# Layer 1's two inner PReLUs as max(y, alpha y) in one VectorE step instead of relu on ScalarE plus a VectorE step

## The chip, the cores and the metric

The kernel runs on one core of a Trainium2 chip. The metric is the device time of that core in microseconds, from repeated executions. All runs in this document gave correct results, and none was in the slow state, with one caveat: the single timed run of one experiment (an unchanged kernel, looked at once) has no known state. The profile is one further execution, taken with the hardware profiler, so its span (1042.2 us before) is near the timed median, not equal to it. The granted clock is the share of TensorE's full clock that the chip allowed, as the profiler recorded it; a drop is a fall of it from 1.00 to 0.50.

## The reference, cut to what matters

The program is four layers on 16 images of 256 channels and 28 x 28 pixels. Layer 0 is a binary convolution with batch norm, layer 2 has two binary convolutions, layer 3 is attention. The change is in layer 1 alone:

```python
def prelu(x, alpha):
    return jnp.where(x >= 0, x, _pc(alpha) * x)      # all alphas are 0.25 here

residual = prelu(x, a_alpha1)
z = hardsign(x + _pc(a_move))
y = conv3x3(z, a_w)                                   # cut
y = prelu(bn(y, a_bn1), a_alpha2)                     # inner PReLU 1
mix = s * x + y * (1.0 - s)
y = se_gate(mix, ...) * y
y = bn(y * residual, a_bn2) + residual
res2 = y
u = conv1x1(hardsign(y + _pc(f_move)), f_w)           # cut
u = prelu(bn(u, f_bn1), f_alpha2)                     # inner PReLU 2
mix2 = s2 * y + (1.0 - s2) * u
u = bn(se_gate(mix2, ...) * u, f_bn2)
return u + res2
```

`se_gate` needs the mean of each channel over the image: mean, a small product (below "hid"), relu, another small product ("gate"), sigmoid. So the gate of an image cannot be computed before the PReLU of all its channels is done.

## The kernel before

Channels lie on the 128 partitions in two blocks, so a block of an image is a tile of 128 x 784. The 16 images run through a software pipeline, `iteration(b)`: the 3x3 convolution of image b beside the gates, 1x1 convolution and second PReLU of images b-1 and b-2. In the traces TensorE, VectorE and ScalarE run in the order in which the program names their work: ScalarE's eviction, relu, eviction, relu of `unit_u` and `unit_r` at the end start in that order, 0.9 us apart, from about 484.3 us on before. The kernel has TensorE write a convolution's result to PSUM (tile "cv"); an eviction is the instruction that moves it out of there. The row step (L654) is VectorE's eviction of the 3x3 convolution, which makes y. Each PReLU is two instructions: ScalarE computes r = relu(-y), VectorE computes y + (1 - alpha) r and sums it for the gate.

```python
def relu_neg(ap, bias=0.0, scale=-1.0, apart=False):            # L569
    r = full("rn", "rn", 4)
    ...     # A.activation(r, ap, AF.Relu, bias=bias, scale=scale), in two halves if apart
    return r

def prelu_a(b, mo):
    pairs[b, mo] = relu_neg(ys[b, mo])

def prelu_b(b, mo):                                             # L664
    y = ys[b, mo]
    V.scalar_tensor_tensor(
        y, pairs.pop((b, mo)), ra2[:, mo:mo + 1], y, ALU.mult, ALU.add,
        accum_out=sums_of(b + 1)[1][:, 0, mo:mo + 1],
    )

def unit_u(b, mo, u=None, vector=False):                        # evicts the 1x1 convolution
    ...
    if vector:                                                  # L735
        for h in range(2):
            V.tensor_scalar(halves(u)[:, h], ps[:, h], s3[:, m], c3[:, m], ALU.mult, ALU.add)
    else:                                                       # L737
        A.activation(halves(u), ps, AF.Identity, bias=c3[:, m], scale=s3[:, m])
    us[b, mo] = (u, ps)

def unit_r(b, mo, apart=False):                                 # relu, from PSUM, beside the eviction
    ...
    us[b, mo] = (u, relu_neg(ps, nc3[:, m], ns3[:, m], apart))

def unit_b(b, mo):                                              # L747
    u, r = us[b, mo]
    V.scalar_tensor_tensor(
        u, r, rf2[:, mo:mo + 1], u, ALU.mult, ALU.add, accum_out=sums_of(b + 2)[1][:, 1, mo:mo + 1]
    )
```

After the last image there is no other image's convolution to hide behind, so the two gates of the last image lie bare. The kernel fills these stretches with dummy matmuls (`keep_busy(n)`, tile "unused", L371), so that TensorE does not go quiet. I call what follows the end of layer 1, with a first and a second stage:

```python
# first stage: last branch of iteration(b) of the last image
conv1x1(b - 1)
for k in range(2):
    unit_u(b - 1, k)
    unit_r(b - 1, k)
    unit_b(b - 1, k)
for i, u in enumerate((0, 3)):
    conv_pair(b, 1, i, u)
px = hidden_x(B)
rows_out(b, 1)
prelu_a(b, 1)
prelu_b(b, 1)
...
b = B - 1
keep_busy(14)
g = gates(hidden_b(B, hidden_a(B, px)))
keep_busy(14)
...                                     # product with the residual, sign, conv1x1(b)
# second stage
unit_u(b, 0, last[:, 0, :])
unit_u(b, 1, last[:, 1, :], True)
for k in range(2):
    unit_r(b, k, k == 1)
    unit_b(b, k)
keep_busy(14)
h = hidden_a(B + 1, px)
...                                     # sums for layer 2's batch norm
g = gates(h)[:, 1]
keep_busy(14)
...                                     # in all 26 dummies up to layer 2's first convolution (L285)
```

## Time and profile before

| | before |
|---|---|
| timed runs, median (range) | 1045.65 us (1045.01 to 1046.67, 3 runs) |
| span of the profile | 1042.2 us |
| layer 1 in the profile | about 140 to 515 us |
| one image's period in layer 1 | 21.9 us |
| the end of layer 1, from the last period's gate matmul (474.82) to layer 2's first matmul (515.11) | 40.29 us |

The prediction below shows the engine table, the periods, TensorE's waits and the chain. One more view belongs ahead of it: the groups of instructions by shape, with what the two inner PReLUs cost. The columns are line, engine, operation, out<-in and shapes, count, then total busy us and mean ns of one, then the idle time ahead of them on their engine and what ended it.

```profile
L664 DVE SCALAR_TENSOR_TENSOR y<-rn,ra,y 128x784 f32<-128x784 f32 x32 | 33.0, 1032 | 9.4 <-ACT rn L569 9.3
L569 ACT ACTIVATE rn<-cv,nc,ns 128x784 f32<-128x784 f32 x31 | 31.1, 1004 | 0.0
L747 DVE SCALAR_TENSOR_TENSOR u<-rn,rf,u 128x784 f32<-128x784 f32 x30 | 30.0, 1030 | 4.3 <-ACT rn L569 4.3
L569 ACT ACTIVATE rn<-y 128x784 f32<-128x784 f32 x32 | 27.1, 846 | 10.1 <-DVE y L654 10.1
```

There are about 58 us of relus on ScalarE in these two rows, and about 14 us in which VectorE stood still for them. Whether any of that sets the time is another question, because TensorE is the engine that is never free in the periods (busy for 21.91 of 21.91 us).

### The profile page before, as it was taken

What the parts mean: (1) busy time and instruction counts of PE and PEld (TensorE: products, weight loads), DVE (VectorE), ACT (ScalarE), POOL (GpSimd) and SP (SyncE); (2) the same over time, 40 slices, a digit from 0 to 9 for tenths busy, and PEclk for the clock granted to TensorE, in tenths of its full rate; (3) what the DMA queues carried; (4) which work ended last, traced back from release to release, by engine and by line L of the source; (5) the groups of instructions that cost most, each with busy time, mean ns of one, the idle gap of its engine ahead of it and who ended that gap; (6) DMA issues with size and microseconds to landing.
All of it is one profiled execution on the core that took longest, in us unless ns stands there. A gap on an engine that the chain in (4) does not pass through costs nothing.

```text
span 1042.2 us, 15026 instructions
## 1 busy us (share of the span) xinstructions
PE 1007.5 (97%) x5667; PEld 827.9 (79%) x5667; DVE 826.0 (79%) x1460; ACT 729.8 (70%) x1189; POOL 139.4 (13%) x147
## 2 busy tenths in 40 slices
PE   6999999999999999999999999999999999999995
PEld 6899979999999999997589997999844444444442
DVE  4987588999999999985688887888865777768665
ACT  6888745777777777675777785777676676766652
POOL 2000100000000000000100000000024354443531
PEclk9999999999999999999899999999999999999998
DMA  9755521222332223100464000000013435344312
GB/s 340 235 192 187 199 78 47 93 78 78 108 109 90 81 78 105 66 32 31 176 255 186 1 1 1 1 1 1 1 32 62 95 92 124 68 119 90 97 63 97
DMA packets 24359, 98.77 MB, mean 95 GB/s; under 512 B 3203, under 2 KB 6981, under 8 KB 24277
## 3 DMA queue, kind: packets, MB, share of 16 engines
q1 hardware_dynamic: 18644, 67.17, 18.5%
q0 software_dynamic: 5632, 30.54, 10.8%
q8 instruction: 47, 0.77, 0.3%
q14 instruction: 36, 0.29, 0.1%
HBM read 65.59 MB, written 32.11 MB: 94 GB/s over the span
## 4 chain that ended last, share of the span: by engine, by line
PE 82%; DVE 9%; ACT 6%; issue 1%; DMA 1%; SPq 0%; POOL 0%; ACTq 0%; POOLq 0%; DVEq 0%
PE cv L614 27%; PE cv L285 23%; PE sc L1218 8%; PE av L1239 8%; PE cv L720 4%; PE mi L1195 4%; PE sm L1281 2%; PE mi L1297 2%; DVE ab L296 1%; ACT ab L295 1%; DVE p L1016 1%; PE unused L371 1%; ACT t L294 1%; PE sm L1239 1%; DVE l_parts L515 1%
## 5 line engine op out<-in xcount | busy, mean ns | idle before, releaser
L285 PE MATMUL cv<-fpads,wpk 128*128 128x392 f32 x1728 | 336.6, 356 | 9.2 <-POOL l_fin L152 7.3
L285 PEld LDWEIGHTS cv<-fpads,wpk 128*128 128x128 f32 x1728 | 327.5, 192 | 12.1 <-POOL l_fin L152 7.3
L614 PE MATMUL cv<-vs,w 128*128 128x392 f32 x1536 | 301.1, 354 | 1.4 <-DVE vs L121 1.4
L614 PEld LDWEIGHTS cv<-vs,w 128*128 128x128 f32 x1536 | 287.1, 190 | 3.0 <-issue 1.8
L1222 ACT ACTIVATE es<-sc 128x784 f32<-128x784 f32 x112 | 87.3, 822 | 41.4 <-PE sc L1218 41.4
L296 DVE SCALAR_TENSOR_TENSOR ab<-ab,cv 128x392 f32<-128x392 f32 x96 | 53.9, 561 | 65.8 <-ACT ab L295 65.4
L1218 PE MATMUL sc<-q,keyswa 64*128 64x392 f32 x448 | 90.0, 513 | 0.9 <-ACT es L1222 0.9
L1016 DVE SCALAR_TENSOR_TENSOR p<-ab,vec 128x392 f32<-128x392 f32 x128 | 79.1, 618 | 2.2
L1239 PE MATMUL av<-es,v 128*64 128x392 f32 x448 | 80.8, 499 | 0.0
L294 ACT ACTIVATE t<-cv,rounding 128x392 f32<-128x392 f32 x96 | 55.4, 577 | 27.1 <-PE cv L285 25.6
L1218 PEld LDWEIGHTS sc<-q,keyswa 64*128 64x128 f32 x448 | 38.9, 186 | 44.0 <-issue 17.1
L1232 POOL TENSOR_TENSOR sum<-sum,es 128x784 f32<-128x784 f32 x32 | 67.2, 2101 | 3.1 <-ACT es L1222 0.6
L1239 PEld LDWEIGHTS av<-es,v 128*64 128x64 f32 x448 | 29.4, 136 | 47.3 <-issue 47.0
L121 DVE TENSOR_TENSOR vs<-pad 128x840 fp32r<-128x840 bf16 (+1 forms) x66 | 64.4, 999 | 0.1
L295 ACT ACTIVATE ab<-t,unrounding 128x392 f32<-128x392 f32 x96 | 59.8, 623 | 3.2
L1206 DVE COPY keyswa<-mi 64x392 f32<-64x392 f32 x31 | 16.3, 564 | 52.1 <-ACT q L1202 52.1
L760 POOL DMA_DIRECT2D x2d<-x x16 | 8.6, 536 | 359.4 <-DVE x L754 296.9
L1019 ACT ACTIVATE t<-ab 128x392 f32<-128x392 f32 x64 | 33.5, 523 | 26.6 <-DVE ab L296 26.6
L720 PE MATMUL cv<-z,fw 128*128 128x392 f32 x256 | 48.8, 342 | 0.7 <-ACT z L712 0.7
L737 ACT ACTIVATE u<-cv,c_bn,s_bn 128x784 f32<-128x784 f32 x30 | 30.1, 1005 | 24.4 <-PE cv L720 24.4
L720 PEld LDWEIGHTS cv<-z,fw 128*128 128x128 f32 x256 | 45.8, 188 | 1.5 <-ACT z L712 1.3
L1195 PE MATMUL mi<-p,wqk 128*128 128x392 f32 x124 | 45.3, 506 | 0.3 <-PE unused L371 0.2
(275 smaller groups left out, 1500.0 us busy)
## 6 DMA issues: line engine op xcount, KB each, us to landing
xs<-in_x_dram SPq DMA_DIRECT2D x30, 784.0 KB, 4.8
x2d<-x POOLq DMA_DIRECT2D x16, 784.0 KB, 3.6
out_dram<-p SPq DMA_DIRECT2D x15, 784.0 KB, 3.8
p<-x2d POOLq DMA_DIRECT2D x14, 784.0 KB, 6.9
p<-x2d SPq DMA_DIRECT2D x13, 784.0 KB, 6.9
n0d<-n POOLq DMA_DIRECT2D x16, 392.0 KB, 4.9
n<-n0d SPq DMA_DIRECT2D x16, 392.0 KB, 3.1
st<-in_w_dram SPq DMA_DIRECT2D x12, 384.0 KB, 6.5
```

What stands on the lines that cost most here:

```text
L121: V.tensor_tensor(o, a, b, op)
L285: T.matmul(pss[j][:, n // size, :HN].rearrange("p (a b) -> p a b", b=S), lhsT=w[:, n, t, :], rhs=pads[:, j // 2 % 2, k, r:r + HR, c:c + S] ...
L294: A.activation(t, ps, AF.Identity, bias=rounding, scale=1.0 / PACK)
L295: A.activation(ab[:, 1], t, AF.Identity, bias=unrounding)
L614: T.matmul(ps.rearrange("p (a b) -> p a b", b=S), lhsT=w[:, k, c, u, mo * P:(mo + 1) * P], rhs=vs[:, b % 2, u, k, :, c:c + S], start=(n == 0),
L720: T.matmul(ps[:, h, :HN], lhsT=w[:, k, mo * P:(mo + 1) * P], rhs=z2[b][:, k, h * HN:(h + 1) * HN], start=(k + i == 0), stop=(k + i == 2),)
L1016: V.scalar_tensor_tensor(p, y, alpha[:, mo:mo + 1], y, ALU.mult, ALU.max)
L1195: T.matmul(ps[:, h, :HN], lhsT=wqk[:, k, :], rhs=x[b][:, k, h * HN:(h + 1) * HN], start=(k == 0), stop=(k == 1))
L1218: T.matmul(ps[:, h, :HN], lhsT=chunk[rows], rhs=qs[b][rows], start=True, stop=True)
L1222: A.activation(e, ps[:, :, :HN], AF.Exp, scale=0.125)
L1232: (V if late else nc.gpsimd).tensor_tensor(sums[b, late], sums[b, late], e, ALU.add)
L1239: T.matmul(ps[64 * h:64 * h + 64, :HN], lhsT=w, rhs=e[:, h, :], start=start, stop=stop)
```

## The change

For alpha at most 1, y + (1 - alpha) relu(-y) is max(y, alpha y), which VectorE does in one instruction that reads y twice (L663 after, 1032 ns). ScalarE's 65 relus for the two inner PReLUs go. The intent is to take work from ScalarE, to take one hand-over between engines out of each PReLU, and to shorten the two bare stages at the end. For the last image's second block the eviction goes back from VectorE (two halves) to ScalarE. As max is wrong for alpha above 1, the alphas are added to the values that the kernel checks at run time, and the careful version of the program, which runs if the check fails, keeps the general form.

```diff
-    doubts = const.tile([P, 8 * B + 6], F32, name="doubts")
+    doubts = const.tile([P, 8 * B + 10], F32, name="doubts")
...
+                for i, n in enumerate(("a_alpha2", "f_alpha2")):
+                    nc.gpsimd.tensor_copy(doubts[:, 8 * B + 6 + 2 * i:8 * B + 8 + 2 * i], pv(n))
...
-            def prelu_a(b, mo):
-                pairs[b, mo] = relu_neg(ys[b, mo])
-
-            def prelu_b(b, mo):
-                ...
+            def prelu(y, alpha, beta, mo, total):
+
+                if careful:
+                    V.scalar_tensor_tensor(
+                        y, relu_neg(y), beta[:, mo:mo + 1], y, ALU.mult, ALU.add, accum_out=total
+                    )
+                else:
+                    V.scalar_tensor_tensor(y, y, pv(alpha)[:, mo:mo + 1], y, ALU.mult, ALU.max, accum_out=total)
...   (unit_u loses its vector form, unit_r goes, unit_b calls prelu; the calls of prelu_a and unit_r go)
                 unit_u(b, 0, last[:, 0, :])
-                unit_u(b, 1, last[:, 1, :], True)
-                for k in range(2):
-                    unit_r(b, k, k == 1)
-                    unit_b(b, k)
+                unit_b(b, 0)
+                unit_u(b, 1, last[:, 1, :])
+                unit_b(b, 1)
                 keep_busy(14)
```

More of the change, by code (lines that the diff above doesn't have):

```diff
@@ L462, in forward @@
             cc, zb2 = vtile("cc"), vtile("zb2")
-            ra1, ra2, rf2, ns1, ns3, nc3 = (vtile(q) for q in ("ra1", "ra2", "rf2", "ns1", "ns3", "nc3"))
+            ra1, ra2, rf2, ns1 = (vtile(q) for q in ("ra1", "ra2", "rf2", "ns1"))
             mix_x, mix_y, mix_c = (const.tile([P, 2, 2], F32, name=n) for n in ("mix_x", "mix_y", "mix_c"))
@@ L472, in constants @@
                 nc.gpsimd.tensor_copy(
-                    doubts[:, 8 * B:], vec[:, VECS.index("a1"):VECS.index("a3") + 1, :].rearrange("p i k -> p (i k)")
+                    doubts[:, 8 * B:8 * B + 6], vec[:, VECS.index("a1"):VECS.index("a3") + 1, :].rearrange("p i k -> p (i k)")
                 )
+                for i, n in enumerate(("a_alpha2", "f_alpha2")):
+                    nc.gpsimd.tensor_copy(doubts[:, 8 * B + 6 + 2 * i:8 * B + 8 + 2 * i], pv(n))
                 v = const.tile([P, 4, 2], F32, name="v_bn")
@@ L487, in constants @@
                     V.tensor_scalar(o, pv(q), -1.0, 1.0, ALU.mult, ALU.add)
-                for o, q in ((ns1, s1), (ns3, s3), (nc3, c3)):
-                    V.tensor_scalar(o, q, -1.0, None, ALU.mult)
+                V.tensor_scalar(ns1, s1, -1.0, None, ALU.mult)
                 tt(zb2, c2, pv("f_move"), ALU.add)
@@ L564, in full, with relu_neg @@
                 return ph.tile([P, N], F32, tag=tag, name=name, bufs=bufs)
-            def relu_neg(ap, bias=0.0, scale=-1.0, apart=False):
+            def relu_neg(ap, bias=0.0):
                 r = full("rn", "rn", 4)
-                for i in range(2) if apart else (slice(0, 2),):
-                    A.activation(
-                        r if len(ap.shape) == 2 else halves(r)[:, i], ap if len(ap.shape) == 2 else ap[:, i], AF.Relu,
-                        bias=bias, scale=scale,
-                    )
+                A.activation(r, ap, AF.Relu, bias=bias, scale=-1.0)
                 return r
@@ L657, in rows_out, with prelu_y @@
                     )
-            def prelu_a(b, mo):
-                pairs[b, mo] = relu_neg(ys[b, mo])
-            def prelu_b(b, mo):
-                y = ys[b, mo]
-                V.scalar_tensor_tensor(
-                    y, pairs.pop((b, mo)), ra2[:, mo:mo + 1], y, ALU.mult, ALU.add,
-                    accum_out=sums_of(b + 1)[1][:, 0, mo:mo + 1],
-                )
+            def prelu(y, alpha, beta, mo, total):
[5 more added lines that the diff above has]
+                    V.scalar_tensor_tensor(y, y, pv(alpha)[:, mo:mo + 1], y, ALU.mult, ALU.max, accum_out=total)
+            def prelu_y(b, mo):
+                prelu(ys[b, mo], "a_alpha2", ra2, mo, sums_of(b + 1)[1][:, 0, mo:mo + 1])
             def hidden_x(t):
@@ L727, in conv1x1, with unit_u @@
                     us[b, mo] = ps
-            def unit_u(b, mo, u=None, vector=False):
+            def unit_u(b, mo, u=None):
                 m, ps = slice(mo, mo + 1), us[b, mo][:, :, :HN]
@@ L732, in unit_u @@
                     u = full("yu", f"u{b}_{mo}", 6)
-                if vector:
-                    for h in range(2):
-                        V.tensor_scalar(halves(u)[:, h], ps[:, h], s3[:, m], c3[:, m], ALU.mult, ALU.add)
-                else:
-                    A.activation(halves(u), ps, AF.Identity, bias=c3[:, m], scale=s3[:, m])
-                us[b, mo] = (u, ps)
-            def unit_r(b, mo, apart=False):
-                m = slice(mo, mo + 1)
-                u, ps = us[b, mo]
-                us[b, mo] = (u, relu_neg(ps, nc3[:, m], ns3[:, m], apart))
+                A.activation(halves(u), ps, AF.Identity, bias=c3[:, m], scale=s3[:, m])
+                us[b, mo] = u
             def unit_b(b, mo):
-                u, r = us[b, mo]
-                V.scalar_tensor_tensor(
-                    u, r, rf2[:, mo:mo + 1], u, ALU.mult, ALU.add, accum_out=sums_of(b + 2)[1][:, 1, mo:mo + 1]
-                )
+                prelu(us[b, mo], "f_alpha2", rf2, mo, sums_of(b + 2)[1][:, 1, mo:mo + 1])
             def branch2(b, k, g):
@@ L754, in branch2 @@
                 V.scalar_tensor_tensor(
-                    v, us.pop((b, k))[0], g[:, k:k + 1], v, ALU.mult, ALU.add, accum_out=sum_x2[:, k, b:b + 1]
+                    v, us.pop((b, k)), g[:, k:k + 1], v, ALU.mult, ALU.add, accum_out=sum_x2[:, k, b:b + 1]
                 )
@@ L785, in iteration @@
                     unit_u(b - 2, 0)
-                if one:
-                    prelu_a(b - 1, 1)
                 if two:
-                    unit_r(b - 2, 0)
                     unit_u(b - 2, 1)
-                    unit_r(b - 2, 1)
                 if ahead:
@@ L794, in iteration @@
                 if one:
-                    prelu_b(b - 1, 1)
+                    prelu_y(b - 1, 1)
                 if ahead:
@@ L826, in iteration @@
                         branch1_a(b - 1, k, g[:, 0])
-                prelu_a(b, 0)
                 for i, u in enumerate((1, 2)):
@@ L833, in iteration @@
                     branch1_b(b - 1, 1)
-                prelu_b(b, 0)
+                prelu_y(b, 0)
                 if two:
@@ L856, in iteration @@
                         unit_u(b - 1, k)
-                        unit_r(b - 1, k)
                         unit_b(b - 1, k)
@@ L862, in iteration @@
                     rows_out(b, 1)
-                    prelu_a(b, 1)
-                    prelu_b(b, 1)
+                    prelu_y(b, 1)
                     return px
@@ L927, in forward @@
                 for k in range(2):
-                    products(x2[b][:, k, :], shift[:, k:k + 1], us[b, k][0], sum_uv[:, k:k + 1])
-                squares(us[b, 0][0], 0.0, sum_uu[:, 0:1])
+                    products(x2[b][:, k, :], shift[:, k:k + 1], us[b, k], sum_uv[:, k:k + 1])
+                squares(us[b, 0], 0.0, sum_uu[:, 0:1])
                 V.tensor_scalar(sum_uv, sum_uv, 2.0, None, ALU.mult)
@@ L939, in forward @@
                 g = gates(h)[:, 1]
-                squares(us[b, 1][0], 0.0, sum_uu[:, 1:2])
+                squares(us[b, 1], 0.0, sum_uu[:, 1:2])
                 keep_busy(14)
```

## The prediction

> **What bounds the kernel now.** I read the page's engine table first, then the busy time by stretches, cut at the pieces of the chain of waits, then TensorE's waits in layer 1, and last the chain itself at layer 1's end.
>
> The engine table (busy us, share of the span, instructions):
>
> ```profile
> PE 1007.5 (97%) x5667; PEld 827.9 (79%) x5667; DVE 826.0 (79%) x1460; ACT 729.8 (70%) x1189; POOL 139.4 (13%) x147
> ```
>
> TensorE is busy nearly all the time; ScalarE, from which the change takes work, is only third. But a share of the whole span hides stages, so I cut layer 1 (about 140 to 515 us) into its images. The chain shows the same four pieces of convolution every 21.9 us (9.2, 2.85, 6.81 and 2.39 us), and these are two of those periods and two stretches of the end (columns: length, busy PE, PEld, DVE, ACT, POOL, then granted clock, DMA share, GB/s):
>
> ```profile
> 319.21:341.13 21.92, 21.92 (x121) 21.85 (x122) 20.28 (x39) 16.32 (x23) 0.53 (x1) 1.00 0.28 92
> 363.04:384.95 21.91, 21.91 (x121) 21.84 (x122) 20.27 (x39) 16.33 (x23) 0.53 (x1) 1.00 0.27 93
> 480.00:500.00 20.00, 17.64 (x82) 12.31 (x83) 13.11 (x30) 12.47 (x19) 0.75 (x2) 0.91 0.10 40
> 500.00:515.00 15.00, 13.14 (x59) 6.89 (x58) 11.39 (x46) 11.54 (x22) 1.73 (x6) 0.89 0.44 163
> ```
>
> In a period TensorE is busy for the whole 21.9 us and its weight loads for 21.84; VectorE leaves 1.6 us free and ScalarE 5.6. Between 140 and 479 us TensorE's waits are one line:
>
> ```profile
> PE cv L614 <- DVE vs L121: 1.4, 1, 1.4
> ```
>
> That one is the stage's start. So in the steady part the change has nothing to win: no matmul waits for a PReLU. Only after 480 us does TensorE idle, run dummy matmuls (tile "unused") and lose clock. There the chain of waits (start, length, what) reads:
>
> ```profile
> 489.11 1.08 DVE y L654 x2
> ...
> 490.27 0.87 ACT rn L569
> 491.13 0.03 issue
> 491.16 1.05 DVE y L664 x2
> ...
> 492.65 0.62 PE hid L542 x4
> ...
> 494.47 4.73 PE unused L371 x14
> 499.20 2.88 PE cv L720 x16
> 502.07 0.03 issue
> 502.10 1.29 DVE last L735 x2
> 503.39 0.02 issue
> 503.41 1.25 ACT rn L569 x2
> 504.67 0.03 issue
> 504.69 1.05 DVE last L747 x2
> ...
> 506.35 0.59 PE hid L542 x4
> ...
> 508.14 7.32 PE unused L371 x26
> 515.46 6.84 PE cv L285 x36
> ```
>
> Here both relus (L569) lie on the path: one for the last image's first PReLU, one pair of halves for its second. Each stage then runs through the small gate matmuls and a block of dummies.
>
> [...] The trace has 846 (relu of y), 946 (relu of the residual, one pointer) and 1005 (eviction, two pointers). [...] each relu that goes is worth its row. [...] layer 3's PReLU is already (mult, max) with the same tensor in both places (L1182), 1027 ns for 784 elements; the form removed (L664, mult, add) is 1032. [...] the granted clock is 1.00 until 494 us, 0.50 from about 494.6 to 498.0 and again from about 508.3 to 511.7, both 3.4 us long [...]. Both follow stretches where TensorE has little but the gate matmuls, which are 2 columns wide.
>
> **The change part by part.** Removed on ScalarE: 32 relus of y (32 x 846 ns = 27.1 us) and 31 whole and 2 half relus of the 1x1 convolution (32.4 us), 59.5 of its 729.8 us. VectorE's PReLU stays one instruction of about 1030 ns plus its 82 ns accumulator read, 64 of them, now reading one tensor twice and alpha from the parameter table: no change. The last image's second channel block is evicted by ScalarE (about 1000 ns) and no longer by VectorE in two halves (1.29 us with their overlap). VectorE loses two 0.16 us constants, GpSimd gains two tiny copies, both inside layer 0. Compared engine by engine, TensorE's order is the same, ScalarE has 64 instructions fewer (65 relus go, one eviction comes) and VectorE 4 in each of the two program variants, careful and not, and the count of activation table loads is the same.
>
> Steady part: 59 us off an engine that nobody on TensorE waits for. VectorE's waits for relus there (6.8 us in front of L664) go too, again unseen: 0 us.
>
> End, first stage. The chain's step at 489.11 starts late because VectorE has to finish the previous image's second PReLU, itself held until 487.99 by ScalarE's run of eviction, relu, eviction, relu (four times 0.9 us from 484.37). Without the relus that PReLU is done by about 487.4, and the row step starts when the convolution ends, at 488.55 in place of 489.02: 0.45. Then 0.98 us, from the row step's end at 490.18 to the PReLU's start at 491.16, is the wait for the relu. Offered: 1.4. But TensorE's 14 dummies before the gate matmul run 488.39 to 491.59, so the gate matmul can move only from 492.65 to about 491.55: 1.1 us.
>
> End, second stage. From the 1x1 convolution's end (502.07) to the last PReLU's end (505.74) it is now 1.29 + 1.25 + 1.05 and gaps. After: eviction 1.0 + PReLU 1.03 + gaps, about 2.15 us, so 1.5 less. Again 14 dummies (501.90 to 505.10) hold the gate matmul: 506.35 becomes 505.10 relative to the convolution, 1.25 us.
>
> Sum with the clock behaving as now: 1.1 + 1.25 = 2.35 us. Everything behind (gate, square, table load, statistics) has the same order and shifts along.
>
> Clock. TensorE's quiet stretch before the dummies shrinks from 2.7 us (491.59 to 494.3) to about 1.7, and the second from 2.9 (505.1 to 508.0) to 1.65[...]. Elsewhere in this trace idle gaps of 1.38 (138.5 us) and 1.35 us (639.4) cost no clock. If no drop happens, the 14 dummies of 4.73 us take about 3.1, as their like does at 488.4 (3.20). The 1x1 convolution then waits for its input instead: its first half would be ready at 496.5 and its second at 497.5, so it ends about 499.8 rather than 502.07 and the gain up to there is 2.25, not 1.1. The 26 dummies of 7.32 us become 5.6 (at 216 ns), and the next layer's first matmul is then held by its two sign instructions, about 7.65 us after the gate matmul started, against 8.8 now: 1.15 more. With no drop at all the total is about 1.1 + 1.15 + 1.25 + 1.15 = 4.65 us. I take some 40% of that extra 2.3, because [...] some runs before may lack a drop as well: 2.35 + 0.9 = 3.2 us.
>
> **The rivals.** First: ScalarE's relief speeds up every period. The relus are 3.7 us of each 21.9, and if they held TensorE, 16 periods would give up to 59 us (986 us, faster by 5%). For it: VectorE does wait for them and has 93% load. Against it: TensorE's 21.91 of 21.91. I give it 1%. Second: the wait only changes its name; the dummies and the gate chain are fixed, and the freed 1.4 and 1.5 us vanish in them: about 1045 us. For it: dummies stand in both stages and I have already capped both gains by them; against it: both gate matmuls start over 1 us after their dummies end. Third: VectorE, now without pauses, becomes the bound, or its in-place PReLU straight after the row step waits for that step's writes. Its work per period stays at 20.3 us of 21.9, and it has one instruction fewer at the end, so at most some 0.1 us twice. Fourth: the clock drops stay but fall elsewhere: 1043.3.
>
> **Range and chances.** 1045.65 - 3.2 = 1042.4 us. The three runs before spread over 1.7 us, the clock adds up to 2.3 us, so 1040.0 to 1044.9 should hold it 8 times in 10. Two per cent is 21 us, nine times the sure part: faster 0.01, slower 0.005.
>
> **What would show it.** Periods still 21.91 us with TensorE at 21.91 while ScalarE falls to about 12.6; the relu rows L569 of y and of the convolution gone, the residual's 32 kept; VectorE's PReLU still near 1030 ns; the gate matmuls starting as the dummies end; layer 2's first matmul 2.3 to 4.7 us earlier; all later stages as long as before. Wrong: a period other than 21.9; a PReLU well over 1.03 us; a gate matmul still a microsecond behind its dummies; or a clock drop over a quiet stretch of 1.7 us, which would leave 2.35.

## The result, and the profile after

| | before | after |
|---|---|---|
| timed runs of one call, median (range, runs) | 1045.57 us (1045.01 to 1046.67, 4) | 1041.31 us (1038.64 to 1041.76, 4) |
| ratio, 95% interval | | 0.9953 [0.9934, 0.9971] |
| span of the profile | 1042.2 us | 1039.0 us |

The verdict is "same" (within 2%), with a real gain of half a per cent. Ratios in this document are the mean time of one kernel's fast runs over that of the other's fast runs of the same rounds, so not quite the ratio of the medians quoted.

The two profiles can be cut at four events that both have: the start, layer 0's first eviction, the last period's gate matmul and layer 2's first matmul.

| stretch, us | before | after | difference |
|---|---|---|---|
| start to layer 0's first eviction (L294) | 17.04 | 19.30 | +2.26 |
| to the last period's gate matmul | 457.78 | 457.72 | -0.06 |
| end of layer 1, to layer 2's first matmul | 40.29 | 34.74 | -5.55 |
| layers 2 and 3, to the end | 527.09 | 527.24 | +0.15 |

So the gain is in the end of layer 1, as predicted, and it is 5.55 us there. The first row hides 2.26 of it in this pair of profiles. Nothing ties it to the change: over the twelve profiles of the experiments the first eviction comes anywhere from 15.69 to 18.20 us, from 15.99 to 18.08 where the start is before's and from 16.97 to 18.20 where it is the changed kernel's. TensorE runs about 4 of its first matmuls in a microsecond until 13.4 us before and until 17.3 us after, and only then 7 (4 from 12 to 13 us and 7 from 14 to 15 before; 4 from 16 to 17 and 7 from 18 to 19 after).

The engine table after:

```profile
PE 1005.1 (97%) x5661; PEld 827.2 (80%) x5667; DVE 823.8 (79%) x1456; ACT 681.1 (66%) x1125; POOL 139.8 (13%) x149
```

ScalarE lost 48.7 us of busy time, 64 instructions; VectorE almost nothing. Two periods and the two stretches of the end after (columns as in the prediction):

```profile
321.36:343.28 21.92, 21.92 (x122) 21.78 (x122) 20.20 (x39) 13.27 (x19) 0.53 (x1) 1.00 0.26 92
365.19:387.10 21.91, 21.91 (x122) 21.77 (x122) 20.19 (x39) 13.26 (x19) 0.53 (x1) 1.00 0.26 93
482.00:502.00 20.00, 18.29 (x93) 13.64 (x95) 14.28 (x33) 10.91 (x18) 1.07 (x2) 1.00 0.11 45
502.00:512.00 10.00, 9.34 (x48) 4.88 (x48) 8.57 (x40) 7.99 (x17) 1.05 (x4) 1.00 0.49 177
```

The period is the same to a hundredth although ScalarE has 3.05 us less to do in it. At the end the granted clock is now 1.00 in both stretches, where it was 0.91 and 0.89. TensorE's waits in layer 1 up to 479 us after are again one line, the stage's start:

```profile
PE cv L611 <- DVE vs L121: 1.4, 1, 1.4
```

The groups of the PReLUs after:

```profile
L663 DVE SCALAR_TENSOR_TENSOR y<-y,vec 128x784 f32<-128x784 f32 x32 | 33.0, 1032 | 0.1
L569 ACT ACTIVATE rn<-xs,nbi 128x784 f32<-128x784 f32 x32 | 30.1, 945 | 1.7 <-DVE nbi L337 1.4
L663 DVE SCALAR_TENSOR_TENSOR u<-u,vec 128x784 f32<-128x784 f32 x30 | 29.9, 1035 | 2.1 <-ACT u L732 2.0
```

VectorE's step costs what it did, 1032 and 1035 ns; only the residual's relus are left on ScalarE. The idle time ahead of y's step fell from 9.4 to 0.1 us, and the periods did not notice. The chain of waits at the end of layer 1 after (start, length, what):

```profile
490.82 2.97 PE unused L371 x13
493.79 0.35 PE hid L543 x4
...
494.74 0.62 PE gate L690 x4
...
496.45 1.05 DVE x L704 x2
497.50 0.02 issue
497.52 0.96 ACT z L711
498.48 0.04 issue
498.52 3.36 PE cv L719 x16
501.89 0.23 PE unused L371
502.12 0.05 issue
502.17 2.75 PE unused L371 x12
504.93 0.35 PE hid L543 x4
...
506.48 5.63 PE unused L371 x26
512.11 6.84 PE cv L285 x36
```

No PReLU is left on it. Both gate products ("hid") start where the dummies end. Between the first stage's gate and the 1x1 convolution (L719) the chain now runs through VectorE and ScalarE, and no longer through 14 dummies of 4.73 us at half clock.

How the clock fell before is best seen in stretches of 1 us (the granted clock is the third column from the right). Before:

```profile
493.00:494.00 1.00, 0.39 (x5) 0.30 (x4) 0.00 (x0) 0.51 (x2) 0.00 (x0) 1.00 0.00 0
494.00:495.00 1.00, 1.00 (x7) 0.64 (x8) 0.25 (x2) 0.26 (x2) 0.00 (x0) 0.81 0.00 0
495.00:496.00 1.00, 1.00 (x4) 0.34 (x3) 0.96 (x2) 0.95 (x1) 0.00 (x0) 0.50 0.00 0
499.00:500.00 1.00, 1.00 (x7) 0.97 (x7) 1.00 (x3) 0.49 (x2) 0.21 (x1) 1.00 0.00 0
```

After, the stretch with the same work:

```profile
494.00:495.00 1.00, 0.39 (x5) 0.30 (x4) 0.00 (x0) 0.51 (x2) 0.00 (x0) 1.00 0.00 0
495.00:496.00 1.00, 1.00 (x8) 0.59 (x8) 0.38 (x2) 0.39 (x2) 0.00 (x0) 1.00 0.00 0
496.00:497.00 1.00, 1.00 (x7) 0.46 (x5) 0.96 (x2) 0.83 (x1) 0.00 (x0) 1.00 0.00 0
```

The first line of each is the small gate matmuls; the second has the last of these and the first dummies; the third is dummies alone. Four matmuls touch that microsecond at clock 0.50 and seven at 1.00: in the trace the dummies start 427 and 216 ns apart. The fourth line of before is the 1x1 convolution, with the clock back at 1.00.

My theory after the result: all of the gain is in the two bare stages at the end of layer 1; about half is the shorter chain and half the clock, which no longer falls. The rivals: first, the relief of ScalarE in the periods gives a part; second, the clock is the only cause; third, the clock is no cause at all.

### The profile page after: what moved, and what is told of

The parts are those of the page before. It is cut to its first block, busy times and chain, and to the rows that moved or that the text cites. A ratio compares the mean times of both kernels' runs of the same rounds, so it can differ in the third digit from the quotient of the medians.

```text
span 1039.0 us, 14936 instructions
## 1 busy us (share of the span) xinstructions
PE 1005.1 (97%) x5661; PEld 827.2 (80%) x5667; DVE 823.8 (79%) x1456; ACT 681.1 (66%) x1125; POOL 139.8 (13%) x149
## 4 chain that ended last, share of the span: by engine, by line
PE 84%; DVE 8%; ACT 6%; issue 1%; DMA 1%; SPq 0%; POOL 0%; ACTq 0%; POOLq 0%
PE cv L611 28%; PE cv L285 23%; PE sc L1197 8%; PE av L1218 8%; PE cv L719 4%; PE mi L1174 4%; PE sm L1260 2%; PE mi L1276 2%; DVE ab L296 1%; ACT ab L295 1%; DVE p L995 1%; ACT t L294 1%; PE unused L371 1%; PE sm L1218 1%; DVE l_parts L516 1%
## 5 line engine op out<-in xcount | busy, mean ns | idle before, releaser
L285 PEld LDWEIGHTS cv<-fpads,wpk 128*128 128x128 f32 x1728 | 328.6, 193 | 13.3 <-POOL se L469 7.3
L294 ACT ACTIVATE t<-cv,rounding 128x392 f32<-128x392 f32 x96 | 55.5, 578 | 26.7 <-PE cv L285 23.8
L632 ACT ACTIVATE t<-cv,c_bn,s_bn 128x392 f32<-128x392 f32 x32 | 21.7, 679 | 50.9 <-PE cv L611 50.9
L732 ACT ACTIVATE u<-cv,c_bn,s_bn 128x784 f32<-128x784 f32 x30 | 30.1, 1006 | 30.5 <-PE cv L719 30.5
L719 PE MATMUL cv<-z,fw 128*128 128x392 f32 x256 | 48.8, 341 | 1.0 <-ACT z L711 0.9
L719 PEld LDWEIGHTS cv<-z,fw 128*128 128x128 f32 x256 | 45.7, 188 | 2.2 <-ACT z L711 2.2
```

The lines of the kernel that those rows point to most:

```text
L285: T.matmul(pss[j][:, n // size, :HN].rearrange("p (a b) -> p a b", b=S), lhsT=w[:, n, t, :], rhs=pads[:, j // 2 % 2, k, r:r + HR, c:c + S] ...
L294: A.activation(t, ps, AF.Identity, bias=rounding, scale=1.0 / PACK)
L719: T.matmul(ps[:, h, :HN], lhsT=w[:, k, mo * P:(mo + 1) * P], rhs=z2[b][:, k, h * HN:(h + 1) * HN], start=(k + i == 0), stop=(k + i == 2),)
```

## The experiments

There are twelve runs, most with three or five rounds: nine new kernels, one of them twice, and both kernels again. In the diffs, `direct` is the new form used in the kernel before: `V.scalar_tensor_tensor(y, y, pv(alpha)[:, mo:mo + 1], y, ALU.mult, ALU.max, accum_out=total)`. "End stretch" is the third row of the table above. A quiet stretch is the time from the end of a stage's first dummies to its next dummies, in which TensorE has only the 2-column gate matmuls.

### The end alone, and everything but the end

`end_only` is the kernel before with the new form only at the end:

```diff
                     for k in range(2):
                         unit_u(b - 1, k)
-                        unit_r(b - 1, k)
-                        unit_b(b - 1, k)
+                        direct(us[b - 1, k][0], "f_alpha2", k, sums_of(b + 1)[1][:, 1, k:k + 1])
...
-                    prelu_a(b, 1)
-                    prelu_b(b, 1)
+                    direct(ys[b, 1], "a_alpha2", 1, sums_of(b + 1)[1][:, 0, 1:2])
...
-                unit_u(b, 1, last[:, 1, :], True)
-                for k in range(2):
-                    unit_r(b, k, k == 1)
-                    unit_b(b, k)
+                direct(us[b, 0][0], "f_alpha2", 0, sums_of(b + 2)[1][:, 1, 0:1])
+                unit_u(b, 1, last[:, 1, :])
+                direct(us[b, 1][0], "f_alpha2", 1, sums_of(b + 2)[1][:, 1, 1:2])
```

> The kernel before, with max(y, alpha y) only in the PReLUs that stand after the last image's convolutions: the two 1x1 PReLUs of image 14 and the second-half PReLU of image 15 (first stage), and both 1x1 PReLUs of image 15 with ScalarE evicting both (second stage). 63 - 4 = 59 relus of the steady part stay on ScalarE. My theory (only the end of layer 1 counts): the whole gain of the change, about 4.3 us, so 1041.3 us if the kernel before is at 1045.6; from the start of the last image's first convolution to layer 2's first matmul about 44.5 us, as in the changed kernel, against 50.0 before. Rival (ScalarE's relief in the periods speeds the kernel): within 1 us of before, about 1045.

Measured: 1039.2 us (1038.3 to 1041.12, 8 runs) against 1044.82 us (43 runs), ratio 0.9958 [0.9943, 0.9973]. End stretch 34.75 us, no clock drop. It is the whole gain, with only the relus of the end removed; those of the periods still run.

`steady_only` is the opposite: the new form everywhere except in those places.

```diff
-                if one:
-                    prelu_a(b - 1, 1)
...
-                    unit_r(b - 2, 0)
...
-                    prelu_b(b - 1, 1)
+                    direct(ys[b - 1, 1], "a_alpha2", 1, sums_of(b)[1][:, 0, 1:2])
...     (the same for unit_b(b - 2, k) and prelu_b(b, 0))
```

> The opposite half: max(y, alpha y) in all PReLUs of the periods (images 0 to 14, and the first-half PReLU of image 15), the end as before with its relus. My theory: same as before within 0.7 us (1045.6), periods of 21.91 us, last stretch about 50 us with both drops of the granted clock. Rival (relief in the periods): most of the 4.3 us, 1041 to 1042.

Measured: 1044.73 us (14 runs), ratio 1.0005 [0.9992, 1.0018]. End stretch 40.28 us with both clock drops. So the 60 or so relus in the periods are worth nothing, and the first rival falls.

### The clock apart from the chain

`before_19` keeps every relu and only puts more dummies into the two places ahead of the gate matmuls, so that the quiet stretch is shorter:

```diff
-                keep_busy(14)
+                keep_busy(19)
                 g = gates(hidden_b(B, hidden_a(B, px)))
...
-                keep_busy(14)
+                keep_busy(19)
                 h = hidden_a(B + 1, px)
```

> The kernel before with all its relus, but with 19 instead of 14 dummy matmuls in the two blocks that stand ahead of the gate matmuls at layer 1's end. They end 0.1 to 0.4 us before the gate matmul's input is ready, so they delay nothing, and TensorE's quiet stretches shrink from 2.7 and 2.9 us to about 1.8 and 2.0. Clock theory: the granted clock stays at 1.00 there, and the kernel gains about 1.1 us (first stage, then bound by the 1x1 convolution's input) plus 1.7 us (26 dummies of 5.6 in place of 7.3 us): 1042.8 us. Rival (the clock drop is chance and has nothing to do with the quiet stretch, all of the gain is the shorter chain): 1045.6, drops in the profile as before.

Measured: 1042.48 us (22 runs), ratio 0.9979 [0.9971, 0.9987]; end stretch 37.58 us, no drop. TensorE's timeline in its first and second stage (start, length, engine, line, operation, tiles, count):

```profile
488.52 4.05 PE L371 MATMUL unused<-idle 128*128 128x512 bf16 x18
492.58 0.61 PE L542 MATMUL hid<-g,se 128*128 128x2 f32 x4
...
494.26 3.18 PE L371 MATMUL unused<-idle 128*128 128x512 bf16 x14
...
500.79 4.28 PE L371 MATMUL unused<-idle 128*128 128x512 bf16 x18
505.23 0.58 PE L542 MATMUL hid<-g,se 128*128 128x2 f32 x4 [0.17 <-DVE g L121]
...
506.88 5.77 PE L371 MATMUL unused<-idle 128*128 128x512 bf16 x25
```

The gate matmul comes when it came before (492.58 against 492.65), as the relu is still on the chain. But the dummies behind it take 3.18 us and not 4.87: the quiet stretch is 494.26 - 492.57 = 1.7 us instead of 2.7, and the clock holds. This one edit of two numbers wins 2.71 us of the 5.55, with no change to the PReLU. The remaining 2.84 (37.58 - 34.74) is the shorter chain at held clock. So the second and the third rival fall too.

`after_7` does the reverse: the changed kernel with `keep_busy(7)` in those two places, so that its quiet stretches grow to before's length.

```diff
-                keep_busy(14)
+                keep_busy(7)
                 g = gates(hidden_b(B, hidden_a(B, px)))
...     (and the same in the second stage)
```

> The changed kernel with 7 instead of 14 dummies in the same two blocks, so that the quiet stretches are again 2.7 and 2.9 us as in the kernel before, while the relus stay gone. The gate matmuls may start 0.2 to 0.4 us earlier. Clock theory: the drops of the granted clock to 0.5 come back in both stretches in most executions and cost about 1.1 and 1.9 us less those 0.5: the stretch from the last image's first convolution to layer 2's first matmul is about 47 us, time about 1043.5. Rival: no drops, 1041 us.

Measured: 1040.58 us (12 runs), ratio 0.9966 [0.9952, 0.998]; end stretch 36.31 us. TensorE's timeline:

```profile
488.48 1.46 PE L371 MATMUL unused<-idle 128*128 128x512 bf16 x6
491.13 0.61 PE L543 MATMUL hid<-g,se 128*128 128x2 f32 x4 [1.20 <-DVE g L121]
...
492.81 3.18 PE L371 MATMUL unused<-idle 128*128 128x512 bf16 x14
...
499.35 1.68 PE L371 MATMUL unused<-idle 128*128 128x512 bf16 x6
502.24 0.58 PE L543 MATMUL hid<-g,se 128*128 128x2 f32 x4 [1.20 <-DVE g L121]
...
503.89 7.46 PE L371 MATMUL unused<-idle 128*128 128x512 bf16 x26
```

This is half a miss. Both quiet stretches are 2.87 us long, but only the second cost clock (26 dummies in 7.46 us, and +1.57 us in the end stretch); behind the first, 14 dummies took 3.18. The profiles together suggest a reason, which is my estimate from the times at which the granted clock changed. In before's profile these are 494.63, 498.04, 508.28, 511.69, 552.65, 556.07 and 1033.93 us, whole multiples of 3.413 us apart to within 0.05 us. In each of the six other profiles in which more than one fall was timed, the falls are so too, with another place in each run: `steady_only` falls at 495.42 and 509.07, the second `before` below at 495.26 and 508.92, in both four times 3.413 apart as in before. If I count steps of 3.413 us back from a profile's last fall (1030.53 us in `after_7`'s), `after_7`'s first stretch is cut by a boundary into 1.29 and 1.58 us; its second has 2.42 us within one step. Counted so at the end of layer 1 in 13 of the 14 profiles (all but `relu_twice`'s), no step with up to 1.88 us of quiet was followed by a drop, and each with 2.42 us or more was. So of the stretches of 2.75 to 2.91 us there some cost clock and two did not (`after_7`'s first and one in `stage1_only` below), which by this estimate is luck of the place, and none of the 1.4 us ones did. Before's two stretches end 13.67 us apart, close to four steps, so by the estimate they should drop together; in the three of these profiles that show the end as it was (both of `before`, `steady_only`), both did.

This is no rule for the whole kernel. In layer 2 the clock fell at 552.65 us before and at 549.79 us after, behind a step with only 1.79 and 1.80 us in which TensorE was idle or ran 1-column matmuls ("sumabs"). Before's timeline around its fall:

```profile
546.85 3.66 PE L285 MATMUL cv<-fpads,wpk 128*128 128x392 f32 x18
551.87 0.58 PE L245 MATMUL sumabs<-ones,ab 128*128 128x1 f32 x4 [1.36 <-DVE ab L239]
552.30 5.10 PE L285 MATMUL cv<-fpads,wpk 128*128 128x392 f32 x18
```

Eighteen matmuls of one shape take 3.66 us ahead of the second gap and 5.10 behind it, where the clock falls. As 1.88 us of quiet cost nothing at the end of layer 1, the length of the quiet alone does not decide; what else does is open.

### One stage at a time

`stage1_only` takes the first two hunks of `end_only`, `stage2_only` the third.

> The kernel before with max(y, alpha y) only in the first stage of the end: both 1x1 PReLUs of image 14 and the second-half PReLU of image 15. Image 15's own 1x1 PReLUs keep the relus and VectorE's eviction. My theory (each stage gives its own part, through the shorter chain and through the clock drop that its shorter quiet stretch avoids): the gate matmul 1.1 us earlier, the 14 dummies after it at full clock, so the 1x1 convolution ends about 2.4 us earlier than before, the second stage as before with its drop: total about 2.4 us less than before in the profile, ratio about 0.9977. Rival (the first stage's gain is swallowed by the dummies behind it, all of the gain is the second stage's): ratio 0.999 to 1.000.

> The kernel before with the change only in image 15's 1x1 PReLUs (both evicted by ScalarE, max form). My theory: the first stage as before with its drop; gate matmul 1.25 us earlier relative to the 1x1 convolution's end, no drop behind it, 26 dummies in 5.7 us: together about 3.1 us less than before in the profile, ratio about 0.997. The two stages add up to the 5.5 us of the end-only kernel's profile. Rival (first stage holds all): ratio 0.999 to 1.000.

Measured for `stage1_only`: 1040.72 us (6 runs), ratio 0.9958 [0.9943, 0.9974]; end stretch 36.23 us, 4.06 less than before where I had written 2.4. The first drop is gone as expected, but the second, which I had left in, did not come either: the second stretch is still 2.90 us long, and by the same estimate (last fall at 1028.61 us) a boundary cut it into 1.02 and 1.88 us. That would explain this profile. All six timed runs have a mean granted clock of 0.993 to 0.994, so the drop may be rare in this kernel and not only absent from one profile. That is a weak sign, as two timed runs of the changed kernel have 0.991; the question is open. Measured for `stage2_only`: 1042.15 us (8 runs), ratio 0.9969 [0.9959, 0.9979]; end stretch 37.10 us with the first drop alone, so 3.19 less than before, against 3.1 expected. Each stage is worth having by itself, but because of the clock the two are not additive (4.06 + 3.19 against 5.55). No run separates the two parts of the second stage's edit, the max form and the eviction's move from VectorE (1.29 us) to ScalarE (about 1.0 us).

### How much slack had the relus in the periods?

`relu_twice` does each inner relu twice in the kernel before, save at the end. If ScalarE's 5.6 us of idle time in a period were slack, another 3.7 us would vanish in it.

```diff
             def relu_neg(ap, bias=0, scale=-1.0, apart=False):
                 r = full("rn", "rn", 4)
+                if twice[0] and not careful and (len(ap.shape) == 3 or isinstance(bias, int)):
+                    A.activation(halves(r) if len(ap.shape) == 3 else r, ap, AF.Relu, bias=bias, scale=scale)
...     (`twice` becomes False ahead of the first stage of the end)
```

> The kernel before with each relu of the two inner PReLUs issued twice by ScalarE (the second writes the same values again), in the periods of images 0 to 14 and not at the end: 3.7 us more ScalarE work in each period of 21.9 us, so about 20 of 21.9. A probe of how far the removed work is from mattering. My theory (TensorE bounds the periods, ScalarE has 5.6 us free in each): periods still 21.9 us, time within 2 us of before. Rival (ScalarE or VectorE's waits for it are near the bound): periods of 22.5 us or more, 10 us or more slower.

Measured: 1072.77 us (4 runs), ratio 1.0262 [1.0246, 1.0279]. A miss, by 26 us. One period in stretches, then VectorE's longest waits in layer 1 (us in total, times, longest), then TensorE's:

```profile
300.00:323.90 23.90, 22.43 (x121) 21.66 (x121) 20.44 (x39) 19.82 (x28) 0.53 (x1) 1.00 0.24 84
```
```profile
DVE u L751 <- ACT rn L573: 25.9, 15, 1.8
DVE y L668 <- ACT rn L573: 23.8, 30, 2.0
```
```profile
PE hid L542 <- DVE g L121: 12.1, 13, 1.0
PE cv L618 <- DVE y L658: 6.4, 12, 0.9
```

The period grew from 21.91 to 23.89 us, so of 3.7 us added 2.0 came through, and the slack was about 1.7 us, not 5.6. No engine is full: TensorE 22.43 of 23.90, VectorE 20.44, ScalarE 19.82. What fills the period is a loop: ScalarE waits for y, VectorE for ScalarE's relu of y and of u, TensorE for the sums of VectorE and for PSUM that VectorE empties. Idle time in an engine inside such a loop is not slack.

`unread_twice` asks which part of the loop counts: ScalarE's work or VectorE's wait for it. It is the changed kernel with two relus in each old place again, of a constant tile or of the convolution's PSUM, into tiles that nobody reads.

```diff
+            def unread(ap, bias=0.0, scale=-1.0):
+                for _ in range(0 if careful else 2):
+                    r = full("rn", "rn", 4)
+                    A.activation(halves(r) if len(ap.shape) == 3 else r, ap, AF.Relu, bias=bias, scale=scale)
...     (called where prelu_a and unit_r stood)
```

> The changed kernel with ScalarE loaded again, in the periods of images 0 to 14, with two relus per PReLU at the places where the doubled relus stood, but nobody reads their results: those of y read a constant tile, those of the 1x1 convolution its PSUM tile. ScalarE has the same work as in the run with doubled relus (period 23.9 us there, my expectation of 21.9 was wrong), but VectorE waits for none of it. If VectorE's wait for the relu made that period (my new theory: a loop of row step, relus, evictions, PReLUs, gate sums and the next row step[...]), most of the 2 us goes: period 21.9 to 22.4, time within 7 us of the changed kernel. Rival (ScalarE's own load): again 23.9, time about 27 us more.

Measured: 1044.9 us (12 runs), ratio 1.0002 [0.9993, 1.001] to the kernel before, so about 5 us over the changed kernel. From layer 1's first matmul to the last period's gate matmul it takes 340.33 us, against 335.04 in the changed kernel, 0.33 us an image over the 16 images, with 118 relus more in the trace (102 us in all, 62 of 844 ns and 56 of 1006 ns), as many as `relu_twice` has in its periods. So most of `relu_twice`'s 2.0 us is VectorE's wait for the result, and ScalarE's bare load is a small part. The two kernels do not do quite the same ScalarE work (the constant tile is always ready), so I take the division as rough.

### Both kernels again, and a try for a faster one

The profiled start differed by 2.26 us between before and after, so I tried to warm TensorE with 13 dummies ahead of the first loads in the changed kernel, and ran it, and both kernels unchanged, again.

```diff
+    idle = const.tile([P, 512], BF16, name="idle")
+    nc.gpsimd.memset(idle, 0.0)
...
+            keep_busy(13)          # ahead of layer 0's first loads
```

> The changed kernel with 13 dummy matmuls at the kernel's very start, before the first image and weights have landed (the dummy tile is zeroed first), meant to end about 7 us, when the first convolution starts. In the profiles of before and after the convolution runs at about 4 matmuls per us from 7 us until 13.4 (before) or 17.0 us (after), then at 7 per us. Theory [...]: the full rate from about 9 us or earlier, the first eviction at about 16 us instead of 17.0 to 19.3, and 1 to 3 us less than the changed kernel, about 1038.5, with less spread. Rival (weights and loads bound the start): same as the changed kernel.

> The kernel with 13 dummies at the very start again, beside the changed kernel on the same chip: the first time its profile had the first eviction at 15.7 us, but the median of five (1040.22) was no better than the changed kernel's. If the start's gain is real, 1 to 2 us faster than the changed kernel of this call (about 1039.5 against 1041); if not, the same within 0.7 us.

> The changed kernel again, as a second profile and for the spread. No drop of the granted clock at layer 1's end [...], since its quiet stretches are 1.4 us; from the last image's gate matmul to layer 2's first matmul 34.7 us as before; the time differs from the first profile only by the start (first eviction 16.0 to 19.3 us in the profiles so far) and the end. Ratio to before about 0.9955. Rival: the absence of drops was luck, the stretch is 36 to 38 us.

> The kernel before, for a second profile: quiet stretches of 2.7 and 2.9 us at layer 1's end, drops of the granted clock in none, one or both [...]; from the last image's gate matmul to layer 2's first matmul 40.3 us with both drops, 37.2 with none.

| run | median (range, runs) | ratio to before | end stretch | first eviction |
|---|---|---|---|---|
| `warm_start` | 1040.22 (1037.69 to 1041.32, 5) | 0.9955 [0.9940, 0.9969] | 34.75 | 15.69 |
| `warm_again` | 1038.97 (1037.55 to 1041.33, 6) | 0.9942 [0.9928, 0.9956] | 34.76 | 17.71 |
| `after_again` (unchanged) | 1039.73 (1038.76 to 1041.02, 6) | 0.9951 [0.9939, 0.9964] | 34.74 | 18.20 |
| `before_again` (unchanged) | 1044.49 (1 run, state unknown) | | 40.29, both drops | 17.49 |

The end stretch of both kernels repeats to 0.01 us. The warm start is inconclusive. In its first profile the first eviction came earliest of all; in its second the clock had dropped again from 10.97 to 14.38 us, in a pause of TensorE (0.19 us busy from 10 to 11 us), and its six runs fall into two groups, three at 1037.55 to 1037.96 and three at 1039.98 to 1041.33. Its interval overlaps that of the changed kernel in the same call, so no version is shown to beat it.

## Why the prediction was right, and where a term was off

The time on record was 1042.4 us in a range of 1040.0 to 1044.9; it is 1041.3. The mechanism held, step by step. That the time came within 1.1 us is in part luck: the trace's gain at the end is 5.55 us where 3.2 was weighted, and what lies outside the end brought the timed gain of that call to 4.3.

**The periods give nothing.** Right. Periods of 21.91 and 21.92 us before and after, TensorE's waits one line in both, and `steady_only` at 1.0005. But my picture behind it was too simple: I read 5.6 us of ScalarE idle time as room, and `relu_twice` shows 1.7 us. The step stands because TensorE was full, not because ScalarE was free. Also, ScalarE came down to 13.3 us of a period where I wrote 12.6, and by 48.7 us in all where I counted 59.5 less one eviction: its instructions overlap in the trace (four of about 1.0 us start 0.9 us apart from 484.37 us on).

**VectorE's step costs the same.** Right: 1032 and 1035 ns. Layer 3's PReLU, with the same (mult, max) form at 1027 ns, pointed the right way.

**First stage, 1.1 us.** Right: counted from the last period's gate matmul, the gate product "hid" starts 16.60 us later after and 17.83 before, so 1.23; it starts as the dummies end. Up to the end of the 1x1 convolution it is 24.87 against 27.25, so 2.38, where I had 2.25 for the case of no clock drop.

**Second stage, 1.25 us more.** Right: the second "hid" comes at 27.74 against 31.53, so 3.79 in all against 3.5.

**The last term, 1.15 us, was too small.** From the second "hid" to layer 2's first matmul it is 7.00 us against 8.76, so 1.76. I had that matmul held by two sign instructions. In the trace it starts behind the dummies as soon as the first of them (L961, from 510.92) is done.

**The clock term was under-weighted.** This is the larger error. I took 40% of the extra 2.3 us, an estimate of mine, as before might also run without drops. The profiles are clearer than that. The changed kernel's end showed no drop in any profile that leaves it alone (itself, `after_again`, `end_only`, `unread_twice` and both warm starts); its quiet stretches are 1.41 and 1.42 us, shorter even than the 1.7 and 1.65 that I had worked out. And before has both drops in both its profiles, and a mean granted clock of 0.992 or less in 66 of the 76 timed runs of it in the calls of the experiments, which fits drops in most of them, though a mean over a run does not show where the clock fell. The prediction's support for the clock term was also read too narrowly: it named two idle gaps of 1.38 and 1.35 us that cost no clock, but the same trace has the fall at 552.65 us in layer 2, behind a gap of 1.36 us and four 1-column matmuls, and it was not mentioned.

With both put right the sum is 5.55 us in the trace: 2.71 for the clock and 2.84 for the chain at held clock (no run took them in the other order), against 4.65 with no drop at all and 3.2 as weighted. In the timed runs the gain is 4 to 5 us, as the start and later layers move single runs by microseconds: layers 2 and 3 took 529.58 us in `before_19`'s profile, with half clock from 1030.22 us to the end and by its mean clock of 0.991 over 1041.9 us some 7 us more of it ahead of that (my estimate), and 527.1 in before's, with one and from 1033.93.

**The rivals.** The first (relief in every period) was shown false by `steady_only`; its 59 us would have been 5.6%, not 5%. The second (dummies swallow all) was half true: dummies did cap both gains, at 1.23 and about 1.4 us. The third left no mark: VectorE's step follows the row step with 0.1 us of idle time in all. The fourth (drops stay, elsewhere) did not happen.

## What to carry to other kernels

Taking some 60 instructions from ScalarE, for which the bottleneck did not wait, was worth nothing here (ratio 1.0005), and taking the handful that lie in a bare stretch with no other image to hide behind was worth it all (0.9958); look there first. Where TensorE idles for a chain of small steps, look at the length of the quiet stretch: before's two, of 2.75 and 2.90 us, were each followed by 3.41 us at clock 0.50, and those of 1.4 to 1.8 us in the same place by none (layer 2's drops, behind 1.79 and 1.80 us, show that the length alone does not decide it). Here five more dummies in two places won half of the whole gain without touching the arithmetic. And the idle time of an engine inside a loop of hand-overs was no measure of its slack (ScalarE: 5.6 us idle, about 1.7 us of slack); doubling the work measured it.
